# Set-up of a fused convolution, Fourier-mixer and feed-forward kernel: three small row copies issued by GpSimd instead of ScalarE, and unread products that begin later in the plan

## The chip, the cores and the metric

The kernel runs on one core of one Trainium2 chip. The metric is the device time in microseconds (us), the median of several runs; the kernel before takes 4647.31 us (three runs, 4646.46 to 4648.82). The profile is of one execution of 4642.4 us. Engines are called by their names or by the profile's short names: TensorE (PE, and PEld for its weight loads), VectorE (DVE), ScalarE (ACT), GpSimd (POOL) and SyncE (SP). A "q" behind a name (ACTq, SPq) is that engine's sequencer issuing a transfer.

## What is computed

The input is 32 images of 96 channels, 56 x 56 pixels, all float32. One convolution layer and one token-mixing layer follow each other, and no value passes from one image to another:

```python
# layer 0: inverted bottleneck; bn scales and shifts each channel
h = relu(bn1(w1 @ x))            # 96 -> 576 channels
h = relu(bn_dw(dwconv3x3(h)))    # one 3x3 filter for each of the 576 channels
x = x + bn2(w2 @ h)              # 576 -> 96 channels
# layer 1: tokens = pixels
t = to_tokens(x)
h = relu(bn(layernorm(t) @ w1.T))          # 96 -> 192
X = fft(h, axis=tokens)                    # scaled per channel, bias, relu on both parts
y = ifft(relu(X*diag + bias)).real
t = t + bn(y @ w2.T)
t = t + ffn(layernorm(t))                  # 96 -> 384 -> 96, operands rounded to 8-bit floats
```

The batch norms have fixed statistics, so each is one scale and one shift per channel. The set-up of the kernel works them into the weights. The shift of `bn2` is the one that this change touches: 96 numbers that are to be added to every token.

## The kernel before, in words

**Set-up.** Lines 379 to 390 load the constants of the first convolution and clear a few tiles. Lines 442 to 459 fold the first batch norm into `w1T` and the second into `wdw`. What the later stages need is set up by four functions which run as steps among the first image's work: `second` (line 476: scale and shift of `bn2`, then `w2T`), `attention` (489: `watt`), `mixer` (503: `w2a`, two rows of `gd`) and `ffn` (527: the 8-bit weights). Their inputs come by transfers that SyncE issues in the generator `loads` (392), one group for each function: `fetch` steps. Six of the loads repeat one row of DRAM over many partitions (`row`, line 370); in `attention` there are four of them, `a_g1`, `a_v1`, `a_b1` and `a_m1`, 97 partitions of 192 numbers each.

**The rows of the shift.** TensorE adds the shift of `bn2` itself: a product of a column of ones with `shb`, in three bfloat16 rows whose sum is the float32 shift (line 897, once for each of the groups of a front). `second` makes the three rows one after the other: VectorE rounds what is left of the shift to bfloat16 and spreads it over four copies (483), a transfer takes this row into its partition of `shb` (484), and VectorE takes the rounded part off (485). The transfer at line 484 is issued by ScalarE.

**The stages of an image.** An image is cut in two halves of 28 rows. For each half and each of four groups of 128 channels, `unit` (598) expands 96 to 128 channels (TensorE line 615, ScalarE line 625 into `hs`), starts the 3 x 3 filter (`begin`, ScalarE, line 641, into `acc`), makes one or two products on ScalarE (657), adds the other taps on VectorE (668, six or seven instructions), adds the products by accumulating transfers that GpSimd issues (676), and ends with a relu on ScalarE (685). The last 64 channels take another way, on TensorE (`last_channels`, 717 and 753). `front` (863) contracts to 96 channels on TensorE (881, 897, 915), evicts the tokens (928), normalises them on VectorE (825 to 854) and begins the mixing (974 to 1059). `mid` (1067) and `back` (1286) do the Fourier mixing and the feed-forward part, while later halves are already being convolved.

**What sets the order.** The order of the instructions on every engine is written by a planner, `Plan` (154), while the kernel is built. Each step has an engine, a cost in the planner's own microseconds, a due rank, the buffers that it takes and gives, and the steps that it follows. `emit` (222) runs through the planner's own clock and, whenever an engine is idle there, emits the ready step of the lowest rank. What is emitted is then fixed: each engine takes its instructions in that order, and an instruction that has to wait holds up all that stand behind it on its engine. The hardware waits themselves are put in by the framework, by the tiles that instructions touch. Transfers issued by SyncE and by ScalarE share one round of eight completion semaphores, in the order in which the program emits them; a transfer that comes to a semaphore again waits on its own sequencer until the transfer that had it before is complete. Transfers that GpSimd issues have a round of eight of their own.

**Unread products.** If TensorE has nothing ready in the planner's clock and has been busy for less than 75% of its last 3.413 us there, `emit` puts in an unread product: a 128 x 128 product of `ident` with itself into a part of `pw` that nobody reads (lines 271 to 278, 1486). It takes 0.23 of the planner's microseconds. Every one is two passes of TensorE in the trace, since it is float32. Because TensorE is then not idle in the planner's clock, these products also decide which steps it takes up next.

Of the kernel before, what the change touches and what calls it, by code (L numbers as in the profile page):

```python
# [130 lines left out]

SPARSE = 0.75
FILLER = 0.23

OFF = (-4.5, 0.5, 0.5, 8.5)
AT = (3.0, 0.5)
# [6 lines left out]
class Step:  # L143
    def __init__(self, engine, cost, emit, after, take, give, late, rank, at):
        self.engine, self.cost, self.emit = engine, cost, emit
        self.take, self.give, self.late = take, give, late
        self.rank, self.at = rank, at
        self.left = len(after)
        self.next = []
        for a in after:  # L150
            a.next.append(self)


class Plan:
# [58 lines left out]
    def step(self, engine, cost, emit, after=(), take=(), give=(), late=None, rank=None):  # L213
        late = self.LATE.get(engine, 0.1) if late is None else late
        if rank is None:
            rank = self.now
            self.now += self.pace
        s = Step(engine, cost, emit, list(after), list(take), list(give), late, rank, len(self.steps))
        self.steps.append(s)
        return s  # L220

    def emit(self):
        ready = {s.engine: [] for s in self.steps}
        idle = dict.fromkeys(ready, True)
        for s in self.steps:
            if not s.left:
                heapq.heappush(ready[s.engine], (s.rank, s.at, s))
        events, count, left = [(0.0, 0, None, None)], 1, len(self.steps)
        work = sum(s.engine == "PE" for s in self.steps)
        while events:  # L230
            now = events[0][0]
            while events and events[0][0] <= now:
                _, _, engine, s = heapq.heappop(events)
                if engine:
                    idle[engine] = True
                elif s:
                    for b in s.give:
                        self.free[b] += 1
                    for n in s.next:
                        n.left -= 1  # L240
                        if not n.left:
                            heapq.heappush(ready[n.engine], (n.rank, n.at, n))
            for engine, heap in ready.items():
                if not idle[engine]:
                    continue
                passed, wanted = [], set()
                while heap:
                    item = heapq.heappop(heap)
                    s = item[2]
                    short = {b for b in s.take if self.free[b] < s.take.count(b)}  # L250
                    if short or wanted.intersection(s.take):
                        wanted |= short
                        passed.append(item)
                        continue
                    for b in s.take:
                        self.free[b] -= 1
                    s.emit()
                    left -= 1
                    idle[engine] = False
                    cost = self.stretched(now, s.cost) if engine == "PE" else s.cost  # L260
                    if engine == "PE":
                        self.recent.append((now, now + cost))
                        work -= 1
                    late = self.moved(now, s.late) if isinstance(s.late, tuple) else s.late
                    heapq.heappush(events, (now + cost, count, engine, None))
                    heapq.heappush(events, (now + cost + late, count + 1, None, s))
                    count += 2
                    break
                for item in passed:
                    heapq.heappush(heap, item)  # L270
                if engine == "PE" and idle[engine] and work and now > 0 and self.sparse(now):

                    self.filler()
                    idle[engine] = False
                    cost = self.stretched(now, FILLER)
                    self.recent.append((now, now + cost))
                    heapq.heappush(events, (now + cost, count, engine, None))
                    count += 1
        assert not left, "a step waits for a buffer that nothing frees"
# [3 lines left out]
def tile_kernel(ctx: ExitStack, tc: tile.TileContext, d: dict, out: bass.AP):  # L283
    nc = tc.nc
# [18 lines left out]
    def cst(shape, name, dt=F32):  # L303
        return const.tile(shape, dt, name=name, tag=name)
# [32 lines left out]
    shb = cst([3, 4, C], "shb", BF16)  # L337
# [21 lines left out]
    def tmp(p, n, dt=F32):  # L359
        words = n if dt == F32 else n // 2  # L360
        t = next(j for j, v in reversed([*enumerate(scratch)]) if v.shape[0] >= p and used[j] + words <= v.shape[1])
        v = scratch[t][0:p, used[t] : used[t] + words]
        used[t] += words
        return v if dt == F32 else v.bitcast(dt)
# [64 lines left out]
    def scale_of(g, v, p, n):  # L429
        s, r, w = tmp(p, n), tmp(p, n), tmp(p, n)  # L430
        nc.vector.tensor_scalar_add(v, v, EPS)
        nc.scalar.activation(r, v, AF.Sqrt)
        newton(s, r, v, w)
        nc.vector.tensor_mul(s, s, g)
        return s

    def shift_of(o, b, m, s, w):
        nc.vector.tensor_mul(w, m, s)
        nc.vector.tensor_sub(o, b, w)
# [36 lines left out]
    def second():  # L476
        g, v, b, m = given[0]
        s = scale_of(g, v, 128, C)
        sh, rest = tmp(1, C), tmp(1, C)
        shift_of(sh, b, m, s[0:1, :], rest)  # L480
        for n in range(3):
            part = tmp(1, 4 * C, BF16)
            nc.vector.tensor_copy(part.rearrange("p (q c) -> p q c", q=4), sh.unsqueeze(1).to_broadcast([1, 4, C]))
            nc.scalar.dma_start(out=shb[n : n + 1, :, :].rearrange("p q c -> p (q c)"), in_=part)
            nc.vector.tensor_sub(rest, sh, part[:, 0:C])
            sh = rest
        nc.vector.tensor_mul(w2T, w2T, s.unsqueeze(1).to_broadcast([128, NK + 1, C]))
# [83 lines left out]
    for n, (f, count) in enumerate(((second, 7), (attention, 6), (mixer, 21), (ffn, 4))):  # L571
        t = step("SP", 0.55 * count, fetch, sets[-1:], late=(150e3, 170e3, 1.5), rank=-20.0 + n)
        sets.append(step("DVE", 3.0, f, sets[-1:] + [t], rank=14.0 + 4 * n))
# [980 lines left out]
```

## Time and profile before

| what | value |
|---|---|
| time, median of 3 | 4647.31 us |
| span of the profiled execution | 4642.4 us |
| busy: TensorE, VectorE, ScalarE, GpSimd | 4496.0, 4335.3, 4121.2, 339.9 us |
| first instruction of line 668 (VectorE) starts | 36.02 us |
| first eviction of a front, line 928 | 117.4 us |
| time from one image's first eviction to the next one's, images 10 to 30 | 137.5 to 140.6 us |
| transfers of line 484 | three, first issued at 30.10 us |
| unread products in the built program | 931 |

The page gives each engine's busy time for the whole span, a strip of 40 slices of 116 us each, and the groups of instructions that cost most. TensorE, VectorE and ScalarE are all busy in nine tenths or more of nearly every slice from the fifth on. The set-up lies in the first slice alone, so the page hardly shows it; it is read from the timeline of the first 110 us, where each row has a start, a duration, an engine, a line, the tiles and, in brackets, the idle time of that engine before it with what ended it.

### The profile page before, as it was taken

Reading aid. Unit: us, or ns where it says so; the run is one execution under the profiler, and the core shown is the slowest. Engines: PE = TensorE matmul, PEld = TensorE weight load, DVE = VectorE, ACT = ScalarE, POOL = GpSimd, SP = SyncE. Lnnn points to the kernel's source line nnn. Section 1 sums busy time; section 2 is a strip of 40 time slices with the busy share of each in tenths; the row PEclk is TensorE's granted clock in tenths of the full one; section 3 lists DMA queues with packets and bytes.
Section 4 is the critical chain, followed back from the end, with each engine's and each line's share of the span. In section 5 each row is a group of like instructions: output and inputs, shape, how many; then the busy total and the mean of one; then the engine's idle time right before and its main releaser. Section 6 shows DMA issues by size and latency. Waiting matters only on the chain.

```text
span 4642.4 us, 89413 instructions
## 1 busy us (share of the span) xinstructions
PE 4496.0 (97%) x35608; PEld 3351.9 (72%) x35608; DVE 4335.3 (93%) x7053; ACT 4121.2 (89%) x5390; POOL 339.9 (7%) x397
## 2 busy tenths in 40 slices
PE   7999999999999999999999999999999999999998
PEld 4667777777777777777777777777777777777777
DVE  7899999999999999999999999999999999999956
ACT  4677999999999999999999999999999999999854
POOL 0100000000000000000000000000000000000000
PEclk8999999999999999999999999999999999999999
DMA  3577877767877777777767877767776867877753
GB/s 78 130 160 174 192 168 179 183 166 181 187 170 171 187 168 179 185 174 171 184 165 181 187 169 171 187 167 180 187 172 171 187 165 179 191 170 171 170 148 100
DMA packets 390902, 789.51 MB, mean 170 GB/s; under 512 B 135600, under 2 KB 236532, under 8 KB 390484
## 3 DMA queue, kind: packets, MB, share of 16 engines
q1 hardware_dynamic: 335028, 479.15, 37.0%
q0 software_dynamic: 55296, 304.64, 34.1%
q8 instruction: 280, 4.59, 0.4%
q14 instruction: 138, 1.13, 0.1%
q10 hardware_dynamic: 160, 0.01, 0.0%
HBM read 286.38 MB, written 192.68 MB: 103 GB/s over the span
## 4 chain that ended last, share of the span: by engine, by line
PE 56%; ACT 14%; DVE 14%; DMA 5%; issue 3%; SPq 0%; DVEq 0%; ACTq 0%; POOLq 0%
PE pw L881 14%; PE ps L615 9%; DVE acc L668 7%; PE ps L1118 4%; PE ps L1031 3%; PE ps L1000 3%; PE ps L1324 3%; ACT product L657 3%; DMA acc<-product 3%; PE ps L1216 2%; PE ps L753 2%; PE ps L1378 2%; PE pw L915 2%; PE ps L1423 2%; PE ps L717 1%
## 5 line engine op out<-in xcount | busy, mean ns | idle before, releaser
L668 DVE SCALAR_TENSOR_TENSOR acc<-hs,wdw,acc 128x1540 f32<-128x1540 f32 (+2 forms) x1664 | 2972.6, 1793 | 30.1 <-ACT acc L641 22.1
L615 PE MATMUL ps<-xs,w1T 96*128 96x406 f32 x2048 | 805.3, 515 | 18.7 <-ACT hs L625 13.7
L881 PEld LDWEIGHTS pw<-w2T,acc 128*112 128x112 f32 x7168 | 749.4, 178 | 63.6 <-issue 44.5
L881 PE MATMUL pw<-w2T,acc 128*112 128x96 f32 x7168 | 792.8, 264 | 0.5 <-ACT acc L685 0.5
L657 ACT ACTIVATE product<-hs,wdw 128x1568 f32<-128x1568 f32 (+1 forms) x384 | 609.4, 1588 | 17.8 <-DMA product<-product 17.4
L625 ACT ACTIVATE hs<-ps,b 128x812 f32<-128x812 f32 x512 | 478.7, 935 | 114.9 <-PE ps L615 85.1
L615 PEld LDWEIGHTS ps<-xs,w1T 96*128 96x128 f32 x2048 | 363.1, 191 | 251.2 <-issue 177.4
L676 POOL DMA_DIRECT2D acc<-product x256 | 224.6, 877 | 3317.1 <-DVE rf L854 936.7
L641 ACT ACTIVATE acc<-hs,bd,wdw 128x1568 f32<-128x1568 f32 x256 | 435.4, 1701 | 0.2
L685 ACT ACTIVATE acc<-acc 128x1568 f32<-128x1568 f32 x256 | 387.5, 1514 | 42.8 <-DMA acc<-product 42.6
L753 PE MATMUL ps<-hl,band 128*64 128x385 f32 (+3 forms) x3072 | 416.0, 495 | 0.2 <-ACT gc L1258 0.2
L1000 PE MATMUL ps<-watt,xnT 97*120 97x192 f32 x1792 | 334.1, 330 | 16.7 <-DVE V L1147 13.4
L1000 PEld LDWEIGHTS ps<-watt,xnT 97*120 97x120 f32 x1792 | 292.5, 183 | 71.9 <-issue 35.8
L1118 PEld LDWEIGHTS ps<-wb,yb 112*128 112x128 f32 x3528 | 296.6, 165 | 52.2 <-issue 16.0
L1390 ACT ACTIVATE h<-ps 128x784 f16<-128x784 f32 x384 | 315.5, 824 | 15.4 <-PE ps L1378 10.1
L1405 ACT ACTIVATE h<-h 128x784 fp8e5<-128x784 f16 x348 | 298.8, 859 | 34.0 <-DVE h L1396 33.7
L1118 PE MATMUL ps<-wb,yb 112*128 112x112 f32 x3528 | 321.2, 270 | 5.8 <-ACT h L1390 2.5
L1345 ACT ACTIVATE u<-tt,mf,rf 112x96 fp8e5<-112x96 f32 x812 | 315.2, 463 | 0.6 <-DVE mf L857 0.6
L753 PEld LDWEIGHTS ps<-hl,band 128*64 128x64 f32 (+1 forms) x3072 | 152.2, 134 | 209.9 <-issue 180.0
L1486 PE MATMUL pw<-ident 128*128 128x128 f32 x1862 | 268.2, 283 | 3.4 <-ACT xt L928 3.4
L1486 PEld LDWEIGHTS pw<-ident 128*128 128x128 f32 x1862 | 247.4, 197 | 24.9 <-issue 12.5
L1396 DVE TENSOR_SCALAR h<-h,b1q 128x784 f16<-128x784 f16 x384 | 160.2, 418 | 83.9 <-ACT h L1390 81.9
(170 smaller groups left out, 6788.0 us busy)
## 6 DMA issues: line engine op xcount, KB each, us to landing
acc<-product POOLq DMA_DIRECT2D x256, 784.0 KB, 7.3
product<-product POOLq DMA_DIRECT2D x128, 756.0 KB, 10.6
yb<-ydr SPq DMA_DIRECT2D x252, 294.0 KB
wd<-in_wd_dram SPq DMA_DIRECT2D x128, 349.1 KB
wb<-in_wb_dram SPq DMA_DIRECT2D x63, 686.0 KB
ydr<-ya SPq DMA_DIRECT2D x256, 168.0 KB
xs<-in_x_dram SPq DMA_DIRECT2D x64, 609.0 KB
tdr<-xt SPq DMA_DIRECT2D x64, 588.0 KB
```

Of the source, the lines that this page charges most:

```text
L615: nc.tensor.matmul(u[h][:, j, 0:QW], lhsT=w1T[:, 128 * k : 128 * (k + 1)], rhs=xs[img, s][0:C, at : at + QW], start=True, stop=True,)
L625: nc.scalar.activation(flat[:, 2 * h * QW : 2 * (h + 1) * QW].rearrange("p (j w) -> p j w", j=2), u[h][:, :, 0:QW], AF.Relu, bias=b1[:, k ...
L641: nc.scalar.activation(acc[img, s, k], u["hs"][:, o + up : o + up + R, :], AF.Identity, scale=weight(up, 0), bias=bd[:, k : k + 1],)
L657: nc.scalar.activation(u["p", dr][:, ra:rb, :], u["hs"][:, ra + o + dr : rb + o + dr, :], AF.Copy, scale=weight(dr, 0))
L668: nc.vector.scalar_tensor_tensor(dst, src, weight(dr, dc), dst, ALU.mult, ALU.add)
L685: nc.scalar.activation(acc[img, s, k], acc[img, s, k], AF.Relu)
L753: nc.tensor.matmul(pv[:, :, ca:cb], lhsT=band[rows, j, dc + 1, 64 * o : 64 * o + 64], rhs=H[rows, q : q + 7, ca + dc : cb + dc], skip_grou ...
L881: nc.tensor.matmul(u["pw"][0:SK, t, n % 4, 0:C], lhsT=src[rows, (G * t + n) * SK : (G * t + n + 1) * SK], rhs=rhs, skip_group_check=True, **k,
L1000: nc.tensor.matmul(pv[0:PK, q - a, 0:HA], lhsT=xnT[:, q, 0:PK], rhs=watt, start=True, stop=True,)
L1118: nc.tensor.matmul(o, lhsT=lhsT, rhs=u["wb"][:, G * s + q, :], start=True, stop=True)
L1390: nc.scalar.activation(u["h", c].rearrange("p (j w) -> p j w", j=2), u["H", c][:, :, 0:n], AF.Copy)
L1486: nc.tensor.matmul(pw[:, 0, 4 * C :], lhsT=ident, rhs=ident, start=False, stop=False, skip_group_check=True)
```

## The change

Two edits. The three transfers of the shift's rows are issued by GpSimd's queue and not by ScalarE's; GpSimd's accumulating transfers are the only others that it issues. And the planner puts in no unread product before its clock is past 15 us. The first takes three instructions out of ScalarE's stream and leaves the shared round of completion semaphores to SyncE there. The second lets TensorE take up its first real products without having unread ones queued ahead of them; as the planner's clock then runs another way, it also writes another order for what follows.

```diff
 SPARSE = 0.75
 FILLER = 0.23
+FIRST = 15.0
...
-                if engine == "PE" and idle[engine] and work and now > 0 and self.sparse(now):
+                if engine == "PE" and idle[engine] and work and now > FIRST and self.sparse(now):
 
                     self.filler()
...
             nc.vector.tensor_copy(part.rearrange("p (q c) -> p q c", q=4), sh.unsqueeze(1).to_broadcast([1, 4, C]))
-            nc.scalar.dma_start(out=shb[n : n + 1, :, :].rearrange("p q c -> p (q c)"), in_=part)
+            nc.gpsimd.dma_start(out=shb[n : n + 1, :, :].rearrange("p q c -> p (q c)"), in_=part)
             nc.vector.tensor_sub(rest, sh, part[:, 0:C])
```

The added line moves every later line of the kernel down by one: line 484 of the kernel before is line 485 of the changed one.

## The prediction

> **What bounds the kernel now.** I read the page first, then the waits and the timeline of the first 110 us, then the order of the built instructions of both programs, engine by engine. From the page:
>
> ```profile
> span 4642.4 us, 89413 instructions
> PE 4496.0 (97%) x35608; PEld 3351.9 (72%) x35608; DVE 4335.3 (93%) x7053; ACT 4121.2 (89%) x5390; POOL 339.9 (7%) x397
> ...
> DVE  7899999999999999999999999999999999999956
> ACT  4677999999999999999999999999999999999854
> ```
>
> VectorE is the engine to count on: its work is fixed (4335 us), and in images 10 to 30 it idles only 4 to 7 us of each 140. Where it idles much more is the start (7 tenths in slice 1) and the drain at the end. Up to the first eviction of a front (117.4 us) it is idle for 32 us (117.4 less 85.5 busy, by the table of windows). So the question is how many of those 32 us go, and whether they come back later. The waits of the first 110 us:
>
> ```profile
> ACT hs L625 <- DMA shb<-yb: 15.5, 1, 15.5
> PEld ps L615 <- ACT hs L625: 14.1, 1, 14.1
> DVE acc L668 <- ACT acc L641: 13.9, 1, 13.9
> DVE V L308 <- ACT V L432: 8.1, 3, 6.3
> DVE yb L308 <- ACT yb L432: 5.3, 1, 5.3
> ```
>
> These five are two chains. The timeline of the first 40 us shows the longer one (rows of several engines):
>
> ```profile
> 7.84 6.69 PE L1486 MATMUL pw<-ident 128*128 128x128 f32 x48
> ...
> 10.54 0.21 DVE L431 TENSOR_SCALAR V<-V 128x96 f32<-128x96 f32 x1
> 11.22 6.17 SPq L367 DMA_DIRECT2D yb<-in_a_b_dram  x1
> 14.37 5.63 PE L615 MATMUL ps<-xs,w1T 96*128 96x406 f32 x16
> 15.94 0.94 ACT L625 ACTIVATE hs<-ps,b 128x812 f32<-128x812 f32 x1 [11.80 <-PE ps L615]
> 16.77 0.27 ACT L432 ACTIVATE V<-V 128x96 f32<-128x96 f32 x1
> 17.07 0.75 DVE L308 RECIPROCAL V<-V 128x96 f32<-128x96 f32 x1 [6.32 <-ACT V L432]
> ...
> 30.10 2.35 ACTq L484 DMA_DIRECT2D shb<-yb  x3
> 32.50 1.77 ACT L625 ACTIVATE hs<-ps,b 128x812 f32<-128x812 f32 x2 [15.46 <-DMA shb<-yb]
> ...
> 36.02 5.39 DVE L668 SCALAR_TENSOR_TENSOR acc<-hs,wdw,acc 128x1485 f32<-128x1485 f32 x3 [13.91 <-ACT acc L641]
> ```
>
> The 24 unread products (48 passes) hold TensorE until 14.5 us. ScalarE takes its first eviction at 15.94 and, in order, the square root of `second` behind it; VectorE waits 6.32 us for that. ScalarE then stands at line 484 from 17.04 to 30.1 us. The rows it waits to copy were ready at 21.3 (the last line 483), so 9 us of it are not the data. The order with its waits says what: the three transfers come to the shared semaphores 6, 0 and 2, which SyncE's loads of `w2a`, `cw` and `cw` had before them. The trace's semaphore arrivals have the last load of `w2a` complete at 30.3 us, and the row loads `a_g1`, `a_v1`, `a_b1`, `a_m1` at 18.8, 22.3, 25.9 and 29.4. They move at some 21 GB/s, and all later loads stand behind them.
>
> **What the Trainium skill says.** "DMA: Bandwidth & Descriptors", section "Why a DMA increments its semaphore by 16 and not by 1": a SyncE or ScalarE transfer is split over the largest k up to 16 that divides the slowest dimension, so 97 partitions run on one engine, and the other increments are written at once. The trace agrees: each row load shows one early arrival (10.1, 11.6, 17.8, 21.3) and one 8.1 to 10.7 us later, and the rows end some 3.5 us apart. The same page, "Anatomy of one DMA", says that waits sit on the issuing sequencer: here 15.46 us of ScalarE. "TensorE: Matmul & The Clock Gate", section "What's actually happening", has the array at half clock after an idle window of some 3.4 us. Before, the clock fell to 0.5 at 24.2 us, 4.2 us after TensorE stopped at 20.0, and came back at 48.1.
>
> **The change, part by part.**
>
> *Unread products.* 24 go from before the first product of line 615. `w1T` is ready when line 456 ends (9.00 + 0.21) and `xs` landed at 8.3, so line 615 begins at 9.3 rather than 14.37. In the new ScalarE order the root of `second` stands ahead of the first eviction: L431 ends at 10.75, root 10.8 to 11.1, so VectorE's 6.32 us shrink to 0.4. `second` then takes its 5.05 us (17.07 to 22.12 before) and ends at 16.15.
>
> *Row copies.* ScalarE goes straight on. Three evictions at the pace of line 615 (0.34 us for each of four passes, 1.37 for an eviction's product) end at 14.6; line 641 (1.69) ends at 16.3. VectorE's first tap: 16.3, not 36.02. GpSimd waits for line 483 until about 16 and issues three transfers, by its own row (877 ns) some 3 us. Behind them on its queue stands the first accumulation, which needs products not made before 27, so this costs nothing. The copies are first read by line 897, past 85 us. I could not see how long a small GpSimd copy takes beside the row loads: with their data done by 29.4 anything from 2 to 15 us leaves 50 us to spare, so both ends cost nothing.
>
> *New order, new wait.* VectorE now has only two taps (1.715 us each: 22.29 us for 13 at 39.65) ahead of `attention`, where it had 15. They end at 19.75. Queued behind `attention` is every other tap, and on TensorE line 497 of it stands ahead of unread products and the bands of line 753. `attention` waits for `a_v1` (22.3). From there: L431 0.25, root 0.35 and 0.1 of hand-over, to the reciprocal at 23.05; it takes 1.39 and five instructions 0.39 each: 26.4; memset to line 498 0.86: 27.2 to 27.5; then the wait for `a_m1`, 29.4; the last three took 1.05 (71.87 to 72.92): taps go on at 30.5. If the clock has fallen to half by 9.3, line 615 takes 2.7 us for each eviction and the first tap comes at 20.4, yet the end stays at `a_m1`, 30.5 to 31.5.
>
> Then 13 taps, 22.3 us: 52.8. ScalarE must have begun the units by then. Its stream waits for the bands (line 782): 5.4 us of unread products from 27.1, then about 12 of line 753, done at 45; two evictions and a `begin` more make 52.7, level with VectorE. `mixer` takes 5.73 us as before (95.29 to 101.02): 58.5, with 15 taps done. Before, VectorE was at 101.02 with 28 taps done. The 13 taps between are another 22.3: 80.8. **Lead: 101.0 - 80.8 = 20.2 us.** The other way, by idle time: removed 6.3 - 0.4, 13.9 and the 5.3 of `attention` (its root stood behind evictions), added 2.6 and 1.7 for the rows and 0.4 for the root: 20.4.
>
> *Does it last?* The built orders answer most of this. From image 11 to the end every engine has exactly the same sequence in both programs, unread products too (23 and 11 in turns, 888 in all against 931). The remaining work and its order being equal, a lead at image 11 is a lead at the end. Between lie images 1 to 10 in another order. Before, VectorE idled 12.3 and 9.6 us in the first two and then 4.2 to 7.1, as in the steady state. So there is little left to win and something to lose: I take 2 us off for it.
>
> 4647.3 - 20.2 + 2 = **4629 us**.
>
> **The rivals.**
> *Part of the lead is spent again* in images 1 to 10, by fronts that wait at line 825 for line 928 (14.2 us in five waits up to image 9 before) or by TensorE, which is 97% busy. One us an image: 10 lost, 4637. For: the planner settles otherwise. Against: TensorE is idle for some 45 of the first 355 us and ScalarE for 130, so neither is full where the lead is carried.
> *The wait only moves*: `attention` and the bands stand earlier on TensorE and ScalarE waits for line 782; if the fourth unit and `mixer` slip by 15, 5 are left: 4642. Against: the row loads end by 29.4 and all set-up loads by 43.3 in the record of arrivals, and `mixer` is reached at 52.8.
> *Slower*: the new order of ten images costs each the whole spread of idle time seen between steady images, 2.9 us: 29 - 20 = 9 more, or a little above that: 4657. Nothing in the profile speaks for it but that the order is untried.
>
> **How the numbers follow.** Lead kept 0.70; partly spent 0.16; moved 0.10; slower 0.04. Faster by over 0.2% means below 4638.0: the first case, and most of the second, 0.85; same 0.11; slower 0.04. The range runs from the full lead and 7 us of smaller idle in images 1 to 3 (4620) to just past the moved wait (4642).
>
> **What would show it.** After: no idle of ScalarE for the shift's copies; the first tap near 16 (20 at half clock); VectorE waiting twice for row loads between 20 and 30; `mixer` done by about 60; the first eviction of a front near 98 (117.4 less 19); the same 278 us for two images in the steady state. It is wrong if VectorE idles over 25 us before the first front, or if images 1 to 10 take more time than before.

## The result: 4624.4 us, and the profile after

The changed kernel takes 4624.41 us (median of 4 runs, 4623.14 to 4627.15) where the kernel before, beside it, took 4648.07 (4 runs, 4646.46 to 4651.47): a ratio of 0.9949, with an interval of 0.9932 to 0.9966. Timed a second time it took 4628.16 us against 4646.25, a ratio of 0.9958 (0.9945 to 0.9970). The ranges given with ratios are 95% intervals. So the change takes off about 18 to 24 us. The forecast was 4629.

The page of the kernel after, first with the rows of busy time and then the strips of VectorE and ScalarE:

```profile
span 4622.1 us, 89242 instructions
...
PE 4487.7 (97%) x35522; PEld 3344.5 (72%) x35522; DVE 4334.9 (94%) x7053; ACT 4125.6 (89%) x5390; POOL 340.7 (7%) x400
...
DVE  8899899999999999999999999999999999999956
ACT  5778899999999999999999999999999999999854
```

VectorE does the same 4335 us of work in a span 20 us shorter. In its strip the first digit is 8 instead of 7, and the fifth is 8 instead of 9; that one lies in image 4, of which more below. ScalarE's first two digits have gone from 46 to 57. TensorE has 8 us less of work: there are 43 fewer unread products in the built program (888 and 931).

The waits of the first 110 us after, from all engines:

```profile
POOL shb L485 <- DVE yb L486: 10.7, 1, 10.7
...
DVE acc L669 <- ACT acc L642: 4.3, 2, 2.7
...
DVE V L309 <- ACT V L433: 1.6, 3, 0.9
DVE yb L439 <- DMA yb<-in_a_m_dram: 1.4, 1, 1.4
```

ScalarE's 15.5 us for the shift's rows are gone from the list. GpSimd now makes that kind of wait, for data and not for a semaphore, and no engine waits for its copies. VectorE's 13.9 us for its first tap have become 2.7 (4.3 in two waits). Its 8.1 us for roots have become 1.6, and its 5.3 us in `attention` 0.9. New is the 1.4 us for the row `a_m1`.

The timeline of the start, rows of several engines (start, duration, engine, line; in brackets the idle time before and what ended it):

```profile
9.06 9.66 PE L616 MATMUL ps<-xs,w1T 96*128 96x406 f32 x20 [1.08 <-DVE w1T L456]
...
11.02 0.75 DVE L309 RECIPROCAL V<-V 128x96 f32<-128x96 f32 x1 [0.35 <-ACT V L433]
12.17 0.94 ACT L626 ACTIVATE hs<-ps,b 128x812 f32<-128x812 f32 x1 [1.19 <-PE ps L616]
...
14.66 0.94 ACT L626 ACTIVATE hs<-ps,b 128x812 f32<-128x812 f32 x1 [1.55 <-PE ps L616]
...
18.73 3.59 DVE L669 SCALAR_TENSOR_TENSOR acc<-hs,wdw,acc 128x1485 f32<-128x1485 f32 x2 [2.67 <-ACT acc L642]
...
29.61 0.36 DVE L439 TENSOR_TENSOR yb<-yb 97x192 f32<-97x192 f32 x1 [1.42 <-DMA yb<-in_a_m_dram]
30.66 22.36 DVE L669 SCALAR_TENSOR_TENSOR acc<-hs,wdw,acc 128x1485 f32<-128x1485 f32 x13
```

Line 616 begins at 9.06 instead of 14.37; VectorE starts the root's reciprocal at 11.02 instead of 17.07 and its first tap at 18.73 instead of 36.02. `attention` ends with the row `a_m1` that came at 29.6, and the taps go on at 30.66. `mixer` is done at 58.35 with 15 taps done before it. The 28th tap ends at 80.71, where the kernel before was at 101.02 with as many: 20.3 us ahead.

Whether that lead lasts is read from the table of windows, cut at the first eviction of the first front, at that of the twelfth image (image 11) and at the end. The columns are the stretch and its length, then busy us of PE, PEld, DVE, ACT and POOL, and the clock and transfer shares. Before:

```profile
0.00:117.20 117.20, 86.25 (x484) 58.40 (x484) 85.28 (x115) 52.00 (x50) 9.29 (x21) 0.83 0.38 78
117.20:1596.70 1479.50, 1437.93 (x11331) 1068.70 (x11332) 1408.24 (x2128) 1315.61 (x1684) 116.50 (x133) 1.00 0.73 172
1596.70:4642.40 3045.70, 2971.86 (x23795) 2224.84 (x23793) 2841.78 (x4812) 2753.55 (x3659) 214.09 (x244) 1.00 0.72 173
```

And after:

```profile
0.00:98.10 98.10, 76.89 (x448) 53.35 (x448) 84.87 (x122) 51.95 (x50) 10.88 (x23) 0.91 0.45 93
98.10:1577.00 1478.90, 1438.55 (x11281) 1065.67 (x11282) 1408.44 (x2121) 1318.77 (x1685) 116.30 (x133) 0.99 0.73 172
1577.00:4622.10 3045.10, 2972.28 (x23795) 2225.48 (x23793) 2841.61 (x4812) 2754.89 (x3659) 213.47 (x244) 1.00 0.72 173
```

The first stretch is 19.1 us shorter with the same work of VectorE (85.28 and 84.87). The second differs by 0.6 us, the third by 0.6. The whole gain is made before the first front, and VectorE's idle time there has gone from 31.9 to 13.2 us.

### The profile page after: what moved, and what is told of

Read it like the earlier page. It is cut to its first block, busy times and chain, and to the rows that moved or that the text cites. A ratio compares the mean times of both kernels' runs of the same rounds, so it can differ in the third digit from the quotient of the medians.

```text
span 4622.1 us, 89242 instructions
## 1 busy us (share of the span) xinstructions
PE 4487.7 (97%) x35522; PEld 3344.5 (72%) x35522; DVE 4334.9 (94%) x7053; ACT 4125.6 (89%) x5390; POOL 340.7 (7%) x400
## 4 chain that ended last, share of the span: by engine, by line
PE 58%; DVE 13%; ACT 11%; DMA 4%; issue 3%; SPq 0%; DVEq 0%; ACTq 0%; POOLq 0%
PE pw L882 14%; PE ps L616 10%; DVE acc L669 7%; PE ps L1119 4%; PE ps L1032 4%; PE ps L1001 3%; PE ps L1325 3%; PE ps L754 2%; ACT product L658 2%; PE ps L1217 2%; PE ps L1379 2%; DMA acc<-product 2%; PE pw L916 2%; PE ps L1424 2%; PE ps L718 1%
## 5 line engine op out<-in xcount | busy, mean ns | idle before, releaser
L658 ACT ACTIVATE product<-hs,wdw 128x1568 f32<-128x1568 f32 (+1 forms) x384 | 609.4, 1589 | 13.7 <-DMA product<-product 13.2
L1001 PE MATMUL ps<-watt,xnT 97*120 97x192 f32 x1792 | 336.8, 332 | 18.5 <-DVE V L1148 13.8
L1487 PE MATMUL pw<-ident 128*128 128x128 f32 x1776 | 252.3, 280 | 1.4 <-ACT xt L929 1.4
L1487 PEld LDWEIGHTS pw<-ident 128*128 128x128 f32 x1776 | 232.3, 193 | 22.5 <-issue 11.5
```

Source lines behind the costliest of these rows:

```text
L658: nc.scalar.activation(u["p", dr][:, ra:rb, :], u["hs"][:, ra + o + dr : rb + o + dr, :], AF.Copy, scale=weight(dr, 0))
L1001: nc.tensor.matmul(pv[0:PK, q - a, 0:HA], lhsT=xnT[:, q, 0:PK], rhs=watt, start=True, stop=True,)
L1487: nc.tensor.matmul(pw[:, 0, 4 * C :], lhsT=ident, rhs=ident, start=False, stop=False, skip_group_check=True)
```

## The experiments

In what follows, "image 3" and the like mean the time from the first eviction of the front of the image ahead to that of the image itself, counted from 0.

Two theories were to be told apart first: that ScalarE stood for shared completion semaphores behind slow loads (and the copies' issuer matters), or that the start was held by the unread products or the old order (and FIRST matters). Then came three further questions: what made the semaphores late, whether a start's lead reaches the end, and what the order of the first images is worth. Each time difference below is against runs of the kernel before on the same chip.

### Each edit alone

The first edit alone; the order of the kernel before stays as it was:

```diff
-            nc.scalar.dma_start(out=shb[n : n + 1, :, :].rearrange("p q c -> p (q c)"), in_=part)
+            nc.gpsimd.dma_start(out=shb[n : n + 1, :, :].rearrange("p q c -> p (q c)"), in_=part)
```

> The first edit alone: line 484 issued by GpSimd, unread products as before. The built order is that of before on every engine, but for the three transfers. Theory (ScalarE stood for the semaphores of slow loads, and the late start of TensorE is a second, smaller cost): line 615 starts at 14.4 us as before, the second eviction near 17 and not 32.5, second ends at 22.1, the first tap is at 22.2 and not 36.0. Everything behind moves by 13.9 us, and the idle 5.3 us of attention may shrink by up to 1.5: 4633 us (14 to 15.5 less than before). Rival (the unread products are the main cost): 3 us less at most. Rival (the GpSimd copies hold up its accumulations): little less than before, with long waits of line 685.

Measured: 4630.11 us against 4646.42, ratio 0.9964 (0.9951 to 0.9976): 16.3 us less. VectorE's timeline:

```profile
16.14 0.75 DVE L308 RECIPROCAL V<-V 128x96 f32<-128x96 f32 x1 [5.30 <-ACT V L432]
...
21.11 25.97 DVE L668 SCALAR_TENSOR_TENSOR acc<-hs,wdw,acc 128x1485 f32<-128x1485 f32 x15
```

The wait for the root stays at 5.30 us, as the 24 unread products are still there. But the first tap comes at 21.11 instead of 36.02 and without a wait. The root of `attention`, which stood behind late evictions for 5.3 us, is now 2.8 us late. `mixer` is done 17.1 us ahead of the kernel before.

The second edit alone, with the copies on ScalarE as before and the order of the kernel after:

```diff
+FIRST = 15.0
...
-                if engine == "PE" and idle[engine] and work and now > 0 and self.sparse(now):
+                if engine == "PE" and idle[engine] and work and now > FIRST and self.sparse(now):
```

> The second edit alone: no unread product in the first 15 us of the plan, line 485 still issued by ScalarE. The built order is that of after. In it the three transfers take over the semaphores of a half of w2T, of xs2 and of a_g1, which before had complete at 9.6, 15.7 and 18.8 us; not those of w2a and cw. Theory (what holds ScalarE is the load that had the semaphore): ScalarE stands until about 19.5, the first tap is near 24 and not 18.7, attention ends near 35 and not 30.7, so 4 us more than after: 4628 us. Rival (a copy that ScalarE issues stands until all row loads are through, 30 us, in any order): first tap at 36, 4640 to 4648 us.

Measured: 4632.66 us against 4646.42, ratio 0.997 (0.996 to 0.9981): 13.8 us less. The timeline shows ScalarE still standing, but for half as long:

```profile
13.98 5.50 ACTq L485 DMA_DIRECT2D shb<-yb  x3
...
19.53 2.60 ACT L626 ACTIVATE hs<-ps,b 128x812 f32<-128x812 f32 x3 [8.47 <-DMA shb<-yb]
...
23.89 3.59 DVE L669 SCALAR_TENSOR_TENSOR acc<-hs,wdw,acc 128x1485 f32<-128x1485 f32 x2 [7.76 <-ACT acc L642]
```

In this order the copies are emitted earlier, so they come to semaphores which earlier loads had, the last of them `a_g1`. That load completes at 18.90 us in the record of semaphore arrivals, ScalarE's wait for its semaphore ends at 18.94, and ScalarE goes on at 19.53. So the second edit takes away part of the same wait as the first, by moving the copies in the round. That is why 16.3 and 13.8 do not add up to 30. The expected 4628 was too low: the stand delays the evictions, TensorE waits for them (3.62 us) and then runs at half clock from 19.5 to 39.9 us, `attention` waits 3.69 us for its products, and the taps go on at 37.57 instead of 30.66. This profile is of the slowest of the seven runs (4640.05 us), so its times say less than those of the other runs.

### The old order, with the products left out

Here GpSimd issues the copies, and the planner counts the 24 early unread products without emitting them. The order of all other instructions is thus that of the kernel before:

```diff
-FILLER = 0.23
+FILLER = 0.23; FIRST = 15.0
...
-                    self.filler()
+                    if now > FIRST: self.filler()
...
-            nc.scalar.dma_start(out=shb[n : n + 1, :, :].rearrange("p q c -> p (q c)"), in_=part)
+            nc.gpsimd.dma_start(out=shb[n : n + 1, :, :].rearrange("p q c -> p (q c)"), in_=part)
```

> Line 484 issued by GpSimd, and the 24 unread products of the plan's first 15 us counted by the planner but not emitted: TensorE begins early, the order of everything else is that of before. Against e1 it shows the early start alone, against after the order alone. Theory: line 615 from 9.1, first eviction 12.2, the root of second behind it at 13.1 to 13.4, second ends at 18.5, first tap at 18.8: 3.4 us ahead of e1, 4630 us. If the rest of the gain of after lies in where attention stands in the order, that remains missing here (5 us of idle time at its root). If the order of images 1 to 10 that after has costs something, e3 is not slower than after.

Measured: 4626.06 us against 4646.42, ratio 0.9953 (0.994 to 0.9965), 20.4 us less: as much as the change as a whole. The first tap starts at 18.39, `mixer` is done 19.3 us ahead, and the first front comes at 97.7 us (98.1 after the change). So the new order is not needed for the gain. What the second edit adds to the first comes from the products alone: without them the first tap is 2.7 us sooner (18.39 and 21.11) and the first front 2.5 (97.7 and 100.2). The timed runs of the two differ by 4.1 us, with overlapping intervals, so this smaller part is shown by the traces alone.

### What held the semaphores

The loads `a_g1` to `a_m1` are taken over 112 partitions instead of 97 in the kernel before. The 15 more rows are not read:

```diff
-        rows = [row(q, n, HA, C + 1) for n in ("a_g1", "a_v1", "a_b1", "a_m1")]
+        rows = [row(q, n, HA, SK)[0 : C + 1] for n in ("a_g1", "a_v1", "a_b1", "a_m1")]
```

> The kernel before, with the four row loads of attention over 112 partitions and not 97 (the added rows are not read); everything else the same. Theory (one DMA engine carries the row loads, and the loads behind them hold the semaphores that line 484 needs): on 16 engines the rows are through by 18 us, the load of w2a completes before 21, ScalarE stands at line 484 only until the data are there (21.3), the copies are issued by 23.7, first tap near 27.3: 8.7 us less, 4639 us. Rival (a copy on ScalarE's queue is slow in itself): ScalarE stands until 30 as before, 4647 us.

Measured: 4635.19 us against 4646.42, ratio 0.9977 (0.9966 to 0.9987): 11.2 us less, without either edit. The issues of line 367 by SyncE show it (count; shortest, median and longest duration in ns; first and last start):

```profile
L367 SPq DMA_DIRECT2D w2a<-in_a_w2T_dram x3: 361/476/594, 14.6 to 15.5; - x3
...
L367 SPq DMA_DIRECT2D yb<-in_a_b_dram x1: 425/425/425, 9.7 to 9.7; - x1
```

Issuing `a_b1` takes 0.43 us where it took 6.17, and the loads of `w2a` go out from 14.6 where they went out from 24.7. The timeline of ScalarE in the same run:

```profile
19.74 2.00 ACTq L484 DMA_DIRECT2D shb<-yb  x3
...
21.79 1.76 ACT L625 ACTIVATE hs<-ps,b 128x812 f32<-128x812 f32 x2 [4.99 <-DVE yb L485]
```

The copies are issued at 19.74, as soon as VectorE has made the first row, and not at 30.10. The trace also has ScalarE's waits for the three shared semaphores themselves. In the kernel before:

```profile
L484 ACTq EVENT_SEMAPHORE  x3: 17/17/17, 30.0 to 31.9; - x3
```

And with the rows of 112:

```profile
L484 ACTq EVENT_SEMAPHORE  x3: 17/17/17, 17.5 to 21.0; - x3
```

The first of these waits now ends 2.2 us ahead of the data, and before it ended 10 us after them. What is left of ScalarE's stand is 4.99 us, and its releaser is VectorE. So both halves of the theory hold: the semaphores were late since the 97-partition loads were slow, and ScalarE's further wait was for data.

The same edit in the changed kernel:

> The changed kernel with the four row loads of attention over 112 partitions, as in e4. Theory (the lead at the first front is the lead at the end, and what the row loads cost here is 0.2 and 1.4 us of VectorE, of which the later wait for mixer's root on ScalarE, 53.2 us, leaves 0.3): attention ends at 29.3 and not 30.7, mixer begins 0 to 0.4 us sooner, 4626 us, within 1.5 of e5. Rival (the row loads now bound the set-up): 3 us or more less.

Measured: 4628.20 us against 4646.25, ratio 0.9957 (0.9945 to 0.9970). The changed kernel timed beside it took 4628.16, so nothing is gained, as expected, though not by the way expected. In the profiled execution the first tap starts at 16.33, the taps go on at 26.77 and the first front comes at 95.3, 2.6 us ahead of that of the changed kernel beside it (97.9). The earlier first tap goes with TensorE's full clock, which began early in this execution (8.7 us, see the end), and not with the wider rows. Image 4 then takes 143.1 us instead of 136.7 there. And in the order of the kernel before, with the products left out and GpSimd's copies:

> e3 (copies by GpSimd, the 24 leading unread products left out, the order of before) with the row loads over 112 partitions as in e4. Theory: in this order attention comes after 15 taps, at 44 us, when the rows have long landed, so nothing changes against e3: 4626 us, the first front within 1 us of e3's 97.7. Rival (the row loads also hold back the early loads that VectorE or TensorE wait for): 2 us less or more.

Measured: 4623.87 us against 4646.08, ratio 0.9955 (0.9942 to 0.9967), the same as without the wider rows (0.9953). With the copies off ScalarE's queue the slow rows cost nothing that these runs can tell.

### Another issuer

If it is the stand of ScalarE that matters, SyncE could issue the copies as well, at the price of holding up the loads behind them. In the changed kernel:

```diff
-            nc.gpsimd.dma_start(out=shb[n : n + 1, :, :].rearrange("p q c -> p (q c)"), in_=part)
+            nc.sync.dma_start(out=shb[n : n + 1, :, :].rearrange("p q c -> p (q c)"), in_=part)
```

> The changed kernel with the three copies issued by SyncE, in whose order they stand behind the load of xs2 and ahead of watt and of the row loads. Theory (a copy costs what is queued behind it on its issuer): ScalarE is as free as in after, but SyncE stands until VectorE has made the parts, 13.9 to 15.2 us; the row loads are issued from 16.3, a_m1 lands near 31 and not 29.8, attention ends near 32.4: 1.5 us more than e5, 4628 us. Rival (transfers of SyncE and ScalarE are one path, and only GpSimd's is free): back to 4635 or more.

Measured: 4630.87 us against 4646.25, ratio 0.9963 (0.995 to 0.9977), 2.7 us more than the changed kernel beside it (4628.16); the intervals overlap. VectorE's timeline shows where it would come from:

```profile
32.20 0.36 DVE L439 TENSOR_TENSOR yb<-yb 97x192 f32<-97x192 f32 x1 [1.50 <-DMA yb<-in_a_m_dram]
```

The row `a_m1` is there at 32.20 instead of 29.61, because its issue stood behind the copies: it starts at 20.55 us instead of 17.86. `mixer` is done at 60.94 instead of 58.35. So it is not shown that SyncE's copies cost the kernel anything at its end. They too free ScalarE: the kernel is 15.4 us ahead of the one before.

### Does a lead at the start reach the end?

29 instructions on VectorE, which nobody reads, are added at the end of `attention` in the changed kernel. The order of the rest stays:

```diff
+        spin = tmp(128, 512)
+        nc.vector.memset(spin, 0.5)
+        for _ in range(28):
+            nc.vector.scalar_tensor_tensor(spin, spin, 1.0, spin, ALU.mult, ALU.max)
```

> The changed kernel with 29 instructions more on VectorE at the end of attention (a memset and 28 scalar_tensor_tensor over 512 columns of an unread tile; some 15 us, the profile will give the sum). Theory (VectorE sets the end, and time lost or won in its set-up comes out at the end one for one, but for the 1.7 us that it waits later in the first half-image): 13 to 15 us more than e5. Rival (TensorE, 97% busy, sets the end and VectorE has slack over images 1 to 10): 7 us or less.

Measured: 4649.85 us against 4646.25, ratio 1.0007 (0.9999 to 1.0015), 21.7 us more than the changed kernel beside it. That is not the 13 to 15 that were expected, but the load was bigger than was estimated:

```profile
29.95 0.48 DVE L504 MEMSET V<- 128x512 f32 x1 [0.15 <-issue]
30.47 20.31 DVE L506 SCALAR_TENSOR_TENSOR V<-V 128x512 f32<-128x512 f32 x28
```

It is 20.8 us of work, the first front comes 20.5 us later (118.4 and 97.9), and the end 21.7, where the two intervals together allow some 7 us either way (an estimate from their widths). Within that, one microsecond of VectorE ahead of the first front is one microsecond of the kernel in this order.

### The order of the first images

FIRST is the only number in the change. Two other values, with all else as changed; first 25:

```diff
-FIRST = 15.0
+FIRST = 25.0
```

> The changed kernel with the bound at 25 us of the plan in place of 15: 37 unread products fewer before the first front (14 ahead of the bands, 23 before the second half's units), and another order in the images behind. Theory (the start decides, and the order of images 1 to 10 adds or takes a few us that the plan does not foresee): the first front within 1 us of e5, the end within 6 us of it: 4622 to 4634 us. Rival (TensorE's unread products in the set-up cost time by themselves): 3 us less or more of gain, already there at the first front.

Measured: 4638.65 us against 4646.08, ratio 0.9986 (0.9979 to 0.9992), which misses the expectation. The first front comes at 98.7 us, as in the changed kernel. Then image 3 takes 151.0 us (134.5 before the change, 138.9 after it). The waits of all engines in that image (us in total, times, longest):

```profile
DVE sta L826 <- ACT xt L929: 14.8, 2, 9.1
ACT ya L1038 <- PE ps L1032: 14.2, 2, 11.5
```

VectorE stands at line 826 for evictions of a front, and ScalarE, which makes them, stands at line 1038 for TensorE. This is the rival that spends the lead again, from another value of FIRST. TensorE stands there too, 4.45 us up to 413.35 for a transfer, and the record of its clock then has half clock from 413.9 to 424.1: 16 passes of line 882 take 3.30 us, where they took 1.72 just before. And 60, with the same one-line edit:

> The changed kernel with the bound at 60 us of the plan: no unread products ahead of the bands of line 754, 7 and not 48 before the second half's units. Theory as for e9: VectorE's 13 taps and mixer stand where they stood, so the first front is within 2 us of e5 though TensorE reaches the bands 5.8 us sooner; ScalarE now has a line 686 ahead of mixer's root, which can cost 1 to 2 us. The end within 6 us of e5: 4622 to 4634. Rival (unread products cost time by themselves): 5 us less at the first front, and 4623 or less.

Measured: 4621.48 us against 4646.08, ratio 0.9947 (0.9933 to 0.996), the lowest time of all. The first front comes at 98.8 us, no sooner. VectorE's waits at line 826 from 98 to 1600 us add up to 9.6 us here, to 23.9 with FIRST at 15 and to 33.7 with FIRST at 25. The interval overlaps that of the changed kernel, so this value is not shown to be the faster of the two.

### All runs in one view

Lead of the first front and of the first front of image 11 (against 117.2 and 1596.7 us before), VectorE's idle time between the two, and what the timed runs took less than the kernel before. All but the last are from the trace of one execution. From image 11 to the end these traces take 3043.7 to 3051.7 us, so a few us between two of them, or between the second column and the last, say little.

| kernel | lead, first front | lead, image 11 | VectorE idle between | less time, timed |
|---|---|---|---|---|
| before | 0 | 0 | 71.3 | 0 |
| the change | 19.1 | 19.7 | 70.5 | 23.7 |
| the change, second time | 19.3 | 21.4 | 68.8 | 18.1 |
| copies by GpSimd alone | 17.0 | 18.5 | 70.0 | 16.3 |
| FIRST alone | 10.6 | 10.2 | 71.1 | 13.8 |
| old order, products left out | 19.5 | 19.5 | 71.0 | 20.4 |
| the same, rows of 112 | 19.3 | 20.7 | 69.9 | 22.2 |
| before, rows of 112 | 10.9 | 11.5 | 70.8 | 11.2 |
| the change, rows of 112 | 21.9 | 17.5 | 75.5 | 18.1 |
| copies by SyncE | 16.2 | 10.2 | 76.8 | 15.4 |
| load of 20.8 us added | -1.2 | -0.8 | 70.5 | -3.6 |
| FIRST 25 | 18.5 | 6.8 | 83.7 | 7.4 |
| FIRST 60 | 18.4 | 23.7 | 65.1 | 24.6 |

The idle time between explains how far the second column departs from the first: 83.7 is 12.4 more than before, and 18.5 less 12.4 is 6.1 (6.8 measured).

## Why the prediction was right

**The stand of ScalarE.** It was put down to semaphores 6, 0 and 2 behind SyncE's loads and not to the data. Wider rows alone brought the issue to the moment when the data are ready and left only the wait for VectorE. GpSimd's queue took the stand away whole. The arrivals and clock times that the prediction reads lie some 0.25 us late against the timeline, and so does the 117.4 us for the first front (117.2). On the timeline's zero the last load of `w2a` is complete at 30.0 us, ScalarE's wait for its semaphore ends at 30.05, and the copy is issued at 30.10; the clock fell 3.9 us after TensorE stopped, and not 4.2. No conclusion hangs on this. The Trainium skill's "DMA: Bandwidth & Descriptors", section "Why a DMA increments its semaphore by 16 and not by 1", which the prediction used for the 97-partition loads, also has 112 partitions run on 16 engines. This agrees: in the run with wider rows the four loads were complete between 15.0 and 15.7 us and show no early jump of the count, where the slow ones took until 29.1.

**The unread products.** Line 616 was to begin at 9.3 and did at 9.06; the wait for the root was to shrink to 0.4 and is 0.35. Leaving the products out, with the order kept, was worth 2.7 us at the first tap. The prediction's sum, 6.3 less 0.4 for this wait beside 13.9 for the first tap, holds for VectorE's idle time, but it doesn't say how much each edit gives: alone they give 16.3 and 13.8, since each takes away part of the same chain.

**The first tap.** This step was off. It said 16.3, or 20.4 at half clock; measured were 18.73 and, in the second profile of the changed kernel, 19.03. The first evictions are 2.49 us apart (12.17 and 14.66), where 1.37 was taken from the row of before and 2.7 was given as the other end. The products of line 616 took 882 ns each up to 14 us and 502 later, and the record of the granted clock begins its full stretch at 14.27. The pace taken from before was that of a TensorE whose full clock had begun at 10.28, while the unread products still ran. So the edit that lets TensorE begin early also had it begin at half clock, in nine of ten profiles (see the end); the prediction allowed for that only as a clock that had fallen, and here it had not risen yet. As foreseen, nothing followed: `attention` waits for the row `a_m1` either way.

**`attention`.** Taps were to go on at 30.5 and did at 30.66, with waits for two row loads as said, though of 0.22 us for `a_v1` where 2.6 were counted (VectorE had waited 2.67 for its first tap instead) and of 1.42 for `a_m1` where 1.7 were. `mixer` was to be done at 58.5 (58.35), and 28 taps at 80.8 (80.71), so the lead of 20.2 came out as 20.3. The first front was to come near 98 and came at 98.1.

**GpSimd's copies.** They were costed at nothing, for any landing within 2 to 15 us. The three issues took 1.78 us and not some 3, from issue to landing they took 5.0 to 5.1 us, and their first reader, line 898, came at 80.5.

**Images 1 to 10.** The prediction took 2 us off the lead. It should have been nothing here: 1478.9 us against 1479.5. (The timed runs, with 6 to 8 us either way, can't tell the two apart.) But this is a balance and no rule. Image 1 has 8.2 us less of VectorE's idle time than before, and image 4 has 10.0 more. There it waits 6.4 us at line 826 and 1.65 at line 1330 just after it. The rows of TensorE and VectorE in that place:

```profile
545.19 1.72 PE L882 MATMUL pw<-w2T,acc 128*112 128x96 f32 x16
...
549.92 0.49 PE L1205 MATMUL ps<-w2a,eo 64*112 64x96 f32 x2 [3.01 <-ACT hl L741]
...
553.62 3.30 PE L882 MATMUL pw<-w2T,acc 128*112 128x96 f32 x16
...
558.47 0.58 DVE L826 BATCH_NORM_STATS2 sta<-xt 112x6 f32<-112x96 f32 x3 [6.38 <-ACT xt L929]
```

TensorE stands for 3.01 us, the record of its clock has half clock from 550.2 to 557.0, and the same 16 passes of line 882 take 3.30 us instead of 1.72. By these rows, half clock made some 3 of the 6.38 us (an estimate: 1.6 in line 882, and 1.5 in line 1205, whose 26 passes take 2.93 us there, where 28 take 1.54 at 624.97). That the new order has such a place could not be read from the built order. With FIRST at 25 the balance is 12 us the other way, with 60 it is 6 in favour. So the chance given to a partly spent lead was about a real thing, though not about this value. In the thirteen profiles VectorE's idle time in images 3 to 11 goes with TensorE's clock: 48.5 to 49.6 us in the three whose record has no half clock there, 49.0 to 62.9 in the ten with 3.4 to 20.5 us of it, and most in the two with the most (58.4 with 17.1, 62.9 with 20.5). The old order has it too in one execution: with the products left out, image 3 had 10.2 us of half clock and 9.4 of idle time, and with the wider rows none and 5.7. No run changes the clock alone, so how much of the idle time it makes, and why an order lets TensorE stand there for one value of FIRST and not for another, stays open.

**The rivals.** "The wait only moves" fell: `mixer` and the fourth unit came when foreseen. "Slower" fell with the windows. From image 11 on, where the built orders are equal, both kernels took 3045 us in these two profiles.

## What to carry to other kernels

A small transfer on a compute engine's queue can wait for a large load that it has nothing to do with, if both take their completion semaphores from one round: look for idle time of the issuing engine that ends at the transfer, and compare it with when the data were ready. Put such transfers on a queue whose engine has time and a round of its own, or make the load ahead of them quick; here the first took the whole stand away and the second two thirds of it (15.46 us to 4.99). Two edits that shorten the same wait do not add up, and a lead at the start is worth its full size only as far as the order between there and the steady state keeps it.

## What the runs showed that had not been expected

- A load over 97 partitions holds its issuer too, not only its own data. SyncE's issue of `a_b1` lasted 6.17 us and that of `a_m1` 3.43, against 0.43 each over 112 partitions, although these move more bytes (84.0 KB). All loads behind it went out 10 us later.
- It seems that one busy transfer engine is enough to hold a transfer of 768 bytes. Of 16 increments of each copy's semaphore by GpSimd, 14 or 15 came by 16.0, 16.4 and 17.0 us and the last at 19.3, 19.8 and 20.4. In the changed kernel with rows of 112 all 16 of the first came between 17.2 and 17.6. The section of the Trainium skill named above has all 16 engines post an increment for a GpSimd transfer, whatever its shape, which fits; that the late engine is the one that carries the row loads is inferred.
- The moment at which TensorE's full clock begins differs between executions, and the first real products with it. In the changed kernel's two profiles these products took 882 ns each until about 14 us; with rows of 112 nearly all took 502 from the start, and the first tap came 2.4 us sooner (16.33). The record of the granted clock begins with full clock at 14.27 and 14.71 us in the first two and at 8.70 in the third, and in each of the thirteen profiles TensorE's products, unread ones too, are slow up to that moment and quick from it on. (The table of windows gives 1.00 for the time ahead of the first entry, so it does not show this.) With the early unread products the full clock began at 8.2, 9.7 and 10.3 us, without them at 13.1 to 16.0 in nine profiles and at 8.7 in the tenth. The Trainium skill's "TensorE: Matmul & The Clock Gate", section "What's actually happening", has the activity window run freely, so that the moment at which full speed is granted varies. This agrees, though the spread here is wider than the 500 ns either way that it gives.
